# A four-layer network on one core: the third layer's experts are no longer stepped while its gates are computed

## The chip, the cores and the metric

The kernel runs on one core of a Trainium2 chip. The core has five engines with an instruction queue each, worked off in order: TensorE (PE; its weight loads are shown apart as PEld), VectorE (DVE), ScalarE (ACT), GpSimd (POOL) and SyncE (SP), which here only issues DMAs. ACT issues a few DMAs as well. The metric is the device time of one execution in microseconds (us), lower is better. The median of three runs before the change is 3140.76 us (3139.37 to 3149.32).

## The reference, cut to what matters

The network has four layers on x, 4096 tokens of 128 values (in the third layer seen as 4 sequences of 1024, as 4 rows b of 8 tiles of 128 tokens in the kernel). Each layer computes a sequence branch s and a gate branch g from the normalised x:

```python
xn = layernorm(x)
s  = attn(xn)          # layers differ: state space, entmax, rotating state, relative attention
g  = silu(ffn(xn))     # layers differ: fp4, two mixtures of experts, int8
x  = x + s * g
```

Only the third layer (index 2 in the code) is touched. Its sequence branch is a recurrence: per token and head a 2x16 state is turned by an angle, decayed, corrected along a key, and read with a query:

```python
Sd   = rotate(S, ct, st)                    # ct, st from the gates: softplus, tanh, sqrt, ln, exp ...
pred = einsum('bhsd,bhd->bhs', Sd, kt)
S    = Sd + bt * (vt - pred)[..., None] * kt
```

Its gate branch is a mixture of 8 experts (two chosen per token) and a shared expert. An expert is up-projection, relu, square, down-projection. The two branches need nothing of each other until x + s * g.

## The kernel before, in words

**Order of the work.** The program is written with Python generators that are stepped by hand. A list scheduler at build time then gives each engine one fixed order of instructions; what was written earlier has the higher priority, but an instruction may stand ahead of an earlier one whose inputs the scheduler expects later. At run time each queue is strictly in order, so an instruction that waits holds up everything behind it on its engine.

**The third layer** (`layer2`) has these stages, with their times in the profile: projections; the *gates* (`gates2`, from about 1450 us); the *tables* (`chunks2`, the first from 1583 us); the *scan* (`scan2`, its chunks from 1652 to 1995 us); then the output (`out2`) and the fourth layer.

- **Gates** (`gates2`, L1222 on). All gate values of the layer lie in 128x512 tiles. DVE, POOL and ACT hand the tiles to each other in one long chain; then the angles are multiplied up in prefix products (`turn`, L1230 and L1310, L1312 on DVE), and the results transposed. At 16 places it calls `next(beside, None)`.
- **Grams** (`grams2`). Products of neighbouring keys for the first two tables: POOL multiplies (`gram`, L1459), DVE sums (`A`, L1442). POOL also builds decay factors F (L1423, L1427).
- **Experts** (`experts2`, `moe2`). Row by row (b = 0 to 3): load xn (L1049, a DMA issued from ACT's queue, into one buffer), transpose it (xnT: DVE L115, ACT L117), score and choose two experts (ACT L1071; DVE L1072, L193, L194; POOL L197, L198; DVE L199, L201, L1074), and then two halves of 512 tokens. In each half every expert takes one step: POOL weighs the tokens (`xs`, L1083, two buffers), PE transposes (L1090), ACT copies (`xin`, L1092), PE up-projects (L1112), ACT applies Relu and Square in two parts each (`h`, L1113 and L1114), PE down-projects (L1101, L1102). A half ends with the shared expert (`hs`: ACT L1123, POOL L1124), a copy (`gT`, L1130) and Silu (L1134). The generator yields 26 times a row, 104 times in all.
- **Tables** (`chunks2`). For each of four column groups n: keys times decay (`KT`, L1498, on DVE for n = 0 and on POOL after), then seven pairs of large DVE operations (`more`, L1542, and `KT`, L1543). For n = 2 and 3 the grams are made here (POOL L1523, DVE L1513). `KT` and `kh` have one buffer each; DMAs carry the results to memory (`ktd`, `kdd`) and back (`ktc`, `kdc`).
- **Scan** (`scan2`). 128 chunks of 8 tokens, 16 to a tile i. A chunk is four small DVE operations that depend on each other: `prod` L1664, `w` L1667, `step` L1670, `st` L1675. After every second chunk ACT copies the table columns of two chunks into the state tile (`st<-kdc`, L1644, called `bring`; below: the hand-over copy). The copy can start once the `step` of one odd chunk is done and must be done before L1675 of the next odd chunk. Tile by tile the states are then rebuilt: POOL `kt<-kt,w` (L1606), DVE one long scan (`kt<-mz,kt`, L1615), ACT `last` and `mz` (L1617, L1601), POOL `kt<-kt,qt` (L1618), 16 PE matmuls (L1623), ACT `o` (L1625).

**Who steps the experts.** The generator `beside()` in `layer2` (L983) steps `experts` and `grams` once each; `gates2` calls it 16 times. `scan2` gets `experts` itself (as its argument `beside`): it steps it once for each of the nine steps of the first table, then once per chunk, and drains the rest at its end. So before the change the 104 expert steps are written as 16 in the gates, 9 in the first table and 79 in the scan (to chunk 79).

Of the kernel before, what the change touches and what calls it, by code (L numbers as in the profile page):

```python
# [89 lines left out]
def drain(gen):  # L90
    for _ in gen:
        pass
# [838 lines left out]
def layer2(k, W, x_all, eps5, ps, banks, x3, whole, last, I, first):  # L931
# [6 lines left out]
    with tc.tile_pool(name="l2", bufs=1) as keep, tc.tile_pool(name="l2dram", bufs=1, space=DRAM) as dram:  # L938
# [12 lines left out]
        with tc.tile_pool(name="l2g", bufs=1, side="right") as gp:  # L951
            raw = {
                "V": gp.tile([P, 32, 32], F32, tag="V", name="V"),
                "G": gp.tile([P, 7, 32, 16], F32, tag="G", name="G"),
                "N": gp.tile([P, 2, 32, 16], F32, tag="N", name="N"),
            }
            with tc.tile_pool(name="l2p", bufs=1) as p1, tc.tile_pool(name="l2pd", bufs=2) as p2:
                xn = p1.tile([P, NB * NT, D], F32, tag="xn", name="xn")

                def norm(b):  # L960

                    nc.sync.dma_start(out=xr[:, tokens(b), :], in_=x_all[:, tokens(b), :])
                    var, rs = k.layernorm(p2, x_all[:, tokens(b), :], xn[:, tokens(b), :], eps5)
                    nc.sync.dma_start(out=xd[:, tokens(b), :], in_=xn[:, tokens(b), :])
                    ms = p2.tile([P, NT], F32, tag="ms", name="ms")
                    nc.vector.tensor_tensor(ms, var, rs, ALU.mult)
                    nc.vector.tensor_tensor(ms, ms, rs, ALU.mult)
                    nc.vector.tensor_scalar(ms, ms, 1e-6, None, op0=ALU.add)
                    nc.scalar.activation(ms, ms, AF.Sqrt)
                    nc.vector.reciprocal(ms, ms)  # L970
                    return ms

                project2(k, W, p1, p2, ps, xn, norm, rd, szd, kd, qd, raw)
            banks.close()
            ps = PsumTags(banks, tc, {"mm": 3, "tr": "mm", "o": 2, "st": 2, "A": 1}, "ps2s")
            f1 = late.enter_context(tc.tile_pool(name="l2f", bufs=1))
            f2 = late.enter_context(tc.tile_pool(name="l2fd", bufs=2))
            experts = experts2(k, W, f1, f2, ps, xd, gd)
            early = {}
            with tc.tile_pool(name="l2m", bufs=1) as mp, tc.tile_pool(name="l2y", bufs=2) as yp:  # L980
                grams = grams2(k, f1, mp, yp, ps, kd, early)

                def beside():  # L983

                    while True:
                        next(experts, None)
                        next(grams, None)
                        yield

                gates2(k, W, mp, ps, raw, cosp, sinp, outg, coef, beside(), lambda: decays2(k, f1, coef, early))  # L990
                drain(grams)
# [50 lines left out]
def experts2(k, W, p1, p2, ps, xd, gd):  # L1042

    nc = k.nc

    def load(b):
        if b < NB:
            xn = p1.tile([P, NT, D], F32, tag="xn", name="xn")
            nc.scalar.dma_start(out=xn, in_=xd[:, b * NT : (b + 1) * NT, :])  # L1049
            return xn  # L1050

    xn = load(0)
    for b in range(NB):
        xnT = p1.tile([P, T], F32, tag="xnT", name="xnT")
        k.transpose_tiles(ps, "tr", [xn[:, t, :] for t in range(NT)], xnT)
        yield
        g = p1.tile([P, NT, D], F32, tag="g", name="g")
        yield from moe2(k, W, p1, p2, ps, xn, xnT, g)
        xn = load(b + 1)
        nc.scalar.dma_start(out=gd[:, b * NT : (b + 1) * NT, :], in_=g)  # L1060
# [335 lines left out]
def decays2(k, f1, coef, early):  # L1396


    gp = k.nc.gpsimd
    new = lambda name, shape: f1.tile(shape, F32, tag=name, name=name)  # L1400
    m = by_chunks(coef["decay"])
    pre, post, whole = new("pre", [P, 512]), new("post", [P, 512]), new("whole", [P, 512 // CH])
    gp.memset(pre, 1.0)
    gp.memset(post, 1.0)
    for t in range(1, CH):
        gp.tensor_tensor(by_chunks(pre)[:, :, t], by_chunks(pre)[:, :, t - 1], m[:, :, t - 1], ALU.mult)
    gp.tensor_tensor(whole, by_chunks(pre)[:, :, CH - 1], m[:, :, CH - 1], ALU.mult)
    gp.tensor_tensor(pre, pre, coef["scale"], ALU.mult)
    F = factors2(k, f1, coef, slice(0, P))
    for t in range(CH - 2, -1, -1):  # L1410
        gp.tensor_tensor(by_chunks(post)[:, :, t], by_chunks(post)[:, :, t + 1], m[:, :, t + 1], ALU.mult)
    early.update({"pre": pre, "post": post, "whole": whole, "F": F, "f1": f1})
# [18 lines left out]
def grams2(k, f1, p1, p2, ps, kd, early):  # L1431


    nc = k.nc
    early["A"] = []
    waiting = []

    def reduce():

        while waiting:  # L1440
            to, prod = waiting.pop(0)
            k.tc.keep_in_program_order(nc.vector.tensor_reduce(to, prod, AX.X, ALU.add))  # L1442

    for n in range(2):
        bank = (f1 if n else ps).tile([P, NC * CH * (CH - 1) // 2], F32, tag="A", name="A")
        kh = p1.tile([P, 16, P], F32, tag=f"kh{n}", name="kh")
        for hf in range(2):
            fetch2(nc, kh[hf * 64 : hf * 64 + 64], kd, hf * 4 + n)
        yield
        kc = kh.rearrange("p d (c t) -> p c t d", t=CH)  # L1450
        A, end = [], 0
        for u in range(CH - 1):
            left = CH - 1 - u
            A.append(bank[:, end : end + NC * left].rearrange("p (c t) -> p c t", t=left))
            end += NC * left
            for part in range(2):
                cs = slice(part * NC // 2, (part + 1) * NC // 2)
                prod = p2.tile([P, NC // 2, CH - 1, 16], F32, tag="gram", name="gram")[:, :, 0:left, :]
                nc.gpsimd.tensor_tensor(  # L1459
                    prod, kc[:, cs, u + 1 :, :], kc[:, cs, u : u + 1, :].to_broadcast([P, NC // 2, left, 16]), ALU.mult  # L1460
                )
                reduce()
                waiting.append((A[u][:, cs], prod))
            yield
        early["A"].append(A)
    reduce()
    yield
# [926 lines left out]
```

## Time and profile before

The profiled execution took 3140.11 us, of which 3138.4 us are the span of the trace; the 1.7 us between them lie around the span. That execution is 0.65 us under the median of the three runs.

| stretch of the third layer (us) | length | PE | DVE | ACT | POOL |
|---|---|---|---|---|---|
| gates, to the first table's KT (1449.91 to 1582.85) | 132.94 | 44.67 | 98.19 | 47.59 | 98.86 |
| first table, to the first chunk (1582.85 to 1652.12) | 69.27 | 45.55 | 45.77 | 43.16 | 51.92 |
| chunks with tables (1652.12 to 1799.31) | 147.19 | 75.95 | 128.44 | 68.24 | 123.08 |
| chunks 31 to 43 (1799.31 to 1818.45) | 19.14 | 16.84 | 16.86 | 16.52 | 8.40 |
| chunks 44 to 83 (1818.45 to 1916.65) | 98.20 | 71.37 | 67.08 | 62.90 | 54.69 |
| chunks 84 to 127 (1916.65 to 1994.83) | 78.18 | 14.67 | 69.67 | 15.14 | 23.89 |

How to read it: the columns give the busy time of each engine in that stretch, so an engine near the length of its stretch leaves the others little to gain there. Over the whole program no engine is near full (DVE 72%, PE 69%), so the time of a stage is set by who waits for whom. A line of waits reads "engine tile line <- engine tile line: us in total, times, longest"; the instruction on the left stood at the head of its queue until the one on the right was done. A line of the timeline gives start, length, engine, source line, operation, output<-inputs, shapes, count, and in brackets the idle time before it with its releaser. Line numbers in the trace are those of the kernel before.

### The profile page before, as it was taken

The page shows a single profiled execution, that of the slowest core. Times are in us where ns is not written, and L with a number is a line of the kernel's source. Part 1 is how long each engine was busy: PE and PEld are TensorE (multiplying, and loading weights), DVE is VectorE, ACT ScalarE, POOL GpSimd, SP SyncE. Part 2 cuts the span into 40 slices and gives each one's busy share as a digit, 9 for nine tenths or more (in the row PEclk, how much of TensorE's full clock was granted, in tenths as well). Part 3 has the DMA queues.
Part 4 walks back from the last instruction along what each step waited for, and adds up shares of the span by engine and source line. Part 5 has one row for each costly group of instructions (what it writes and reads, how often), then busy time and mean ns, then how long its engine had stood idle before and what let it go on. Part 6 is the DMA issues. An engine that isn't in the chain of part 4 may idle for free. (4 is left out here: it accounts for less than half of the span.)

```text
span 3138.4 us, 48108 instructions
## 1 busy us (share of the span) xinstructions
PE 2160.2 (69%) x17200; PEld 1281.2 (41%) x17201; DVE 2262.5 (72%) x5474; ACT 1565.8 (50%) x3350; POOL 1258.3 (40%) x1154
## 2 busy tenths in 40 slices
PE   5777777577777776794355474456777777877875
PEld 2555555333333232463122232344545544545553
DVE  5555555778888886665868977566788788698777
ACT  3554544333333333434354564136775866775773
POOL 3433434144433335225778853332233332323322
PEclk9888888588888887896555666675766676766666
DMA  3000000100000000222055365448678688678772
GB/s 78 17 1 1 1 1 1 36 0 0 0 0 0 7 7 7 94 96 66 0 143 131 95 175 127 121 134 281 182 240 276 179 261 262 206 239 275 220 246 66
DMA packets 334388, 335.26 MB, mean 107 GB/s; under 512 B 26032, under 2 KB 307500, under 8 KB 328260
## 3 DMA queue, kind: packets, MB, share of 16 engines
q1 hardware_dynamic: 332996, 328.00, 35.6%
q10 hardware_dynamic: 1152, 4.19, 0.4%
q8 instruction: 135, 2.21, 0.3%
q14 instruction: 105, 0.86, 0.1%
HBM read 177.40 MB, written 154.14 MB: 106 GB/s over the span
## 5 line engine op out<-in xcount | busy, mean ns | idle before, releaser
L2252 ACT ACTIVATE neg<-neg,low 128x640 f32<-128x640 f32 (+7 forms) x512 | 390.8, 766 | 102.5 <-DVE low L2245 101.5
L1939 DVE STREAM_TRANSPOSE wT<-neg 128x640 f32<-128x640 f32 (+7 forms) x512 | 366.1, 754 | 51.3 <-PE po L2266 47.7
L2196 POOL TENSOR_SCALAR_AFFINE_SELECT rel<-rel 128x512 f32<-128x512 f32 x288 | 179.8, 635 | 555.1 <-DMA rel<-flat 424.1
L2266 PE MATMUL po<-wT,vb 128*32 128x64 f32 (+1 forms) x10240 | 270.6, 256 | 71.5 <-issue 40.6
L2229 PE MATMUL score<-k,q 32*128 32x512 f32 (+3 forms) x768 | 225.4, 598 | 114.2 <-DVE low L2245 113.5
L2266 PEld LDWEIGHTS po<-wT,vb 128*32 128x32 f32 x10240 | 214.7, 137 | 144.4 <-issue 83.9
L2245 DVE CUSTOM_DVE_ANT_0 neg<-score,rel,low 128x128 f32<-128x128 f32 (+3 forms) x448 | 213.1, 510 | 74.1 <-PE score L2229 33.3
L2167 ACT COPY r<-pr 128x512 f32<-128x512 f32 x256 | 135.2, 584 | 137.9 <-PE pr L2165 96.2
L2245 DVE CUSTOM_DVE_ANT_0 neg<-score,rel 128x512 f32<-128x512 f32 (+3 forms) x320 | 150.7, 520 | 47.1 <-issue 23.2
L2229 PEld LDWEIGHTS score<-k,q 32*128 32x128 f32 x768 | 99.7, 252 | 205.1 <-DVE low L2245 132.8
L2165 PE MATMUL pr<-emb,q 32*128 32x256 f32 x512 | 128.6, 438 | 46.8 <-ACT r L2167 25.8
L840 ACT ACTIVATE h<-pg 128x512 f32<-128x512 f32 x128 | 75.9, 596 | 157.9 <-PE pg L837 154.4
L837 PE MATMUL pg<-xnT,w 128*128 128x512 f32 x256 | 149.3, 667 | 7.0 <-DVE h L841 3.9
L790 POOL TENSOR_TENSOR prod<-rest,kv 128x2048 f32<-128x2048 f32 x32 | 145.2, 4574 | 18.4 <-ACT rest L780 18.4
L839 PE MATMUL pu<-xin,w 128*128 128x512 f32 x256 | 140.6, 632 | 12.9 <-DVE h L841 7.4
L828 PE MATMUL po<-h,w 128*128 128x512 f32 x256 | 129.7, 627 | 26.3 <-DVE h L841 26.3
L2165 PEld LDWEIGHTS pr<-emb,q 32*128 32x128 f32 x512 | 92.3, 270 | 80.2 <-ACT r L2167 38.1
L433 PE MATMUL px<-hT,xbcT 128*128 128x512 f32 x256 | 115.1, 594 | 0.0
L785 DVE TENSOR_REDUCE s<-prod 128x128 f32<-128x2048 f32 x32 | 73.1, 2284 | 49.3 <-POOL prod L790 49.3
L1623 PE MATMUL read<-kt,const_sb 128*128 128x128 f32 x256 | 50.6, 369 | 82.7 <-POOL kt L1618 82.7
L2150 POOL COPY vb<-vr 32x1024 f32<-32x1024 f32 x64 | 66.5, 1040 | 79.8 <-PE po L2266 67.5
L1090 PE MATMUL pt<-ident,xs 128*128 128x128 bf16 x256 | 35.4, 290 | 90.7 <-POOL xs L1083 81.5
(648 smaller groups left out, 5849.4 us busy)
## 6 DMA issues: line engine op xcount, KB each, us to landing
flat<-r SPq DMA_DIRECT2D x128, 512.0 KB
rel<-flat SPq DMA_DIRECT2D x112, 512.0 KB
flat<-r SPq DMA_DIRECT2D x128, 256.0 KB
rel<-flat SPq DMA_DIRECT2D x96, 256.0 KB
kt<-kd SPq DMA_DIRECT2D x16, 512.0 KB
kdc<-kdd SPq DMA_DIRECT2D x16, 512.0 KB
qt<-qd SPq DMA_DIRECT2D x16, 512.0 KB
ktc<-ktd SPq DMA_DIRECT2D x16, 512.0 KB
```

The lines of the kernel that those rows point to most:

```text
L790: nc.gpsimd.tensor_tensor(prod, attn.rearrange("p (t h g) -> p t h g", t=4, g=16)[:, t].unsqueeze(2).to_broadcast(each), kv[:, t, 1, :].re ...
L828: nc.tensor.matmul(po, W["w2"][:, e, c, :], h[:, c, :], start=(e == 0 and c == 0), stop=(e == 7 and c == 1))
L837: nc.tensor.matmul(pg, W["w1"][:, e, c * P : (c + 1) * P], xnT, start=True, stop=True)
L839: nc.tensor.matmul(pu, W["w3"][:, e, c * P : (c + 1) * P], xin, start=True, stop=True)
L1939: nc.vector.transpose(weights[at, pair][j][:, t % 2, 0 : (t + 1) * P], S[j][:, 0 : (t + 1) * P])
L2165: nc.tensor.matmul(to[:, m, :], q[at, t * P : (t + 1) * P], W["emb"][at, i, :], start=True, stop=True)
L2167: nc.scalar.copy(r[:, n], to)
L2196: nc.gpsimd.affine_select(out=rel[:, :, slot(back), :], in_=rel[:, :, slot(0), :], compare_op=op, fill=fill, base=0, pattern=[[0, 4], [-si ...
L2229: nc.tensor.matmul(halves[j // 2][:, j % 2, 0 : last - first], q[at(j), 1 + t * P : 1 + n], kk[at(j), first:last], start=True, stop=True)
L2245: nc.vector.tensor_tensor_reduce(out=neg[:, begin:last], in0=sc[:, begin - first : last - first], in1=rel[:, j, slot : slot + (last - begi ...
L2252: nc.scalar.activation(neg[:, 0:n], neg[:, 0:n], AF.Exp, bias=here, scale=-1.0, accum_out=group["sums"][:, j, t : t + 1])
L2266: nc.tensor.matmul(o[32 * j : 32 * j + 32, 2 * pair + m.start : 2 * pair + 2, :], vb[:, kb % 4 * NT + kb // 4, j].rearrange("p a d -> p (a ...
```

## The change

One line of `beside()` goes. The gates still step the grams at each of their 16 places, but no longer the experts; `scan2` is unchanged and takes the experts from their first step.

```diff
                 def beside():
 
                     while True:
-                        next(experts, None)
                         next(grams, None)
                         yield
```

The same instructions are issued, on the same engines and from the same queues. The 104 expert steps are now written as 9 in the first table and 95 in the scan (to chunk 95). All lines of code behind the deleted one have a number lower by one.

## The prediction

> **What bounds the kernel now.** First read: the busy time by stretch, for the six stretches of the third layer and the few us behind the last.
>
> ```profile
> core 0: us, PE busy (x) PEld busy (x) DVE busy (x) ACT busy (x) POOL busy (x), PEclk, DMA share, GB/s
> 1449.91:1582.85 132.94, 44.67 (x152) 22.04 (x154) 98.19 (x157) 47.59 (x84) 98.86 (x89) 0.55 0.04 9
> 1582.85:1652.12 69.27, 45.55 (x143) 17.05 (x141) 45.77 (x29) 43.16 (x86) 51.92 (x31) 0.57 0.62 160
> 1652.12:1799.31 147.19, 75.95 (x255) 31.40 (x254) 128.44 (x212) 68.24 (x139) 123.08 (x75) 0.62 0.42 107
> 1799.31:1818.45 19.14, 16.84 (x42) 4.39 (x41) 16.86 (x54) 16.52 (x35) 8.40 (x7) 0.73 0.91 308
> 1818.45:1916.65 98.20, 71.37 (x267) 35.73 (x268) 67.08 (x170) 62.90 (x131) 54.69 (x40) 0.65 0.54 122
> 1916.65:1994.83 78.18, 14.67 (x78) 14.10 (x77) 69.67 (x180) 15.14 (x39) 23.89 (x15) 0.58 0.52 115
> ```
>
> In the gates DVE and POOL are both busy for three quarters and ACT for a third: a hand-over chain between DVE and POOL, with expert work in between. From chunk 44 to 83 nothing is full, DVE least of all; once the experts have ended (1916.65) DVE is busy for 89%. So I read DVE's waits, gates first, then first table, then the last 128 chunks.
>
> ```profile
> DVE A L1442 <- POOL gram L1459: 18.4, 6, 5.5
> ...
> DVE more L1542 <- POOL KT L1498: 10.1, 1, 10.1
> DVE xnT L115 <- PE pt L125: 9.9, 1, 9.9
> ...
> DVE st L1675 <- ACT st L1644: 22.0, 9, 5.6
> DVE kt L1615 <- POOL kt L1612: 4.0, 1, 4.0
> ```
>
> The gates wait for POOL, whose queue also holds xs. The scan waits for ACT's hand-over copies, whose queue also holds the experts. How such a wait arises is seen on the timelines of ACT and DVE at 1884 to 1895, and how the scan runs free on ACT's at 1925.
>
> ```profile
> 1884.30 0.57 ACT L1092 COPY xin<-pt 128x512 bf16<-128x512 bf16 x1
> ...
> 1886.77 0.58 ACT L1092 COPY xin<-pt 128x512 bf16<-128x512 bf16 x1
> ...
> 1889.24 0.38 ACT L1644 COPY st<-kdc 128x256 f32<-128x256 f32 x1
> ...
> 1889.66 0.31 DVE L1675 TENSOR_REDUCE st<-step 128x16 f32<-128x144 f32 x1 [5.08 <-ACT st L1644]
> 1894.93 0.31 DVE L1675 TENSOR_REDUCE st<-step 128x16 f32<-128x144 f32 x1 [2.44 <-ACT st L1644]
> ...
> 1925.13 0.38 ACT L1644 COPY st<-kdc 128x256 f32<-128x256 f32 x1 [2.56 <-DVE step L1670]
> 1928.06 0.38 ACT L1644 COPY st<-kdc 128x256 f32<-128x256 f32 x1 [2.55 <-DVE step L1670]
> ```
>
> One expert step takes ACT 2.47 us from one xin to the next (1884.30 to 1886.77). Two free chunks take DVE 2.93 us (1925.13 to 1928.06). So one expert step between two copies fits; two do not.
>
> **A rule for the scan, checked on before.** Let w be ACT's expert work between two neighbouring copies, in the queue's fixed order. A copy takes 0.34 us of the queue. A copy that follows a late one is late by w + 0.34 - 2.93. One that follows a copy in time may use both intervals: late by w - 5.1 (2 x 2.93 less two copies). If a long scan (L1615) falls between, 4.2 us more fit. In the order of before, the stretches of the last row's second half hold 9.73 and 4.98 us: the rule gives 4.6 and 2.4, measured are 5.08 and 2.44. It sizes what follows.
>
> **The change part by part.** The sum is made against the profiled execution (3140.11 us, span 3138.4), 0.65 us under the median.
>
> *Removed from the gates.* By the built order, 13 xs leave POOL (at 1.12 mean, 14.4 us), the top-2 pair (1.09 + 1.59) and a hs pair (2.4): 19.5 us. DVE loses xnT, biased, cmp, eq, rank, two and score (4.2 us) and their waits (1.6 + 1.3 + 1.15). ACT loses eight whole expert steps and more, among them those that held up no one. The bounds: 8 us, if DVE alone sets the pace; 20 us, if POOL does. Walking both queues in the new order with the old durations: reciprocal of det 4 us earlier (alpha no longer waits behind the experts on ACT), reciprocal of mag 11 earlier (the POOL add before it stood behind four xs), the second table's first gram 18 earlier (1525.8 to about 1507.5). From there to the last POOL product (u, 1575.03) the order holds the same work; it ends about 20 earlier. Then 2 to 3 us are given back: KT of the first table now stands behind biased of row 0, which needs transposes, router matmuls and a Sigmoid (3 us from xnT to biased at 1615 to 1618). Gain 18 us.
>
> *Added to the first table.* The DMA that loads row 0 keeps its place early in ACT's queue. Row 0 is routed here instead of row 1, so the wait of 9.9 us for xnT goes, which stood there because row 1's xn is loaded only after row 0 has left the buffer. What is late next: rank waits about 5 us, as POOL does F and kh before the top-2; then the KT of table 1 stands behind ten xs on POOL instead of five. Ten xs at ACT's pace take 17.7 us (as at 1840.98 to 1858), so DVE idles about 11 us before `more`, against 10.1 measured now. First chunk at about 1623 instead of 1652: this stretch gains 10.5. Bounds: the whole idle time of DVE here (22.8) and a loss of 3. SP's queue is shifted with its producers; the new order of its DMAs differs only from table 2 on, and I price that at nothing, since ktc and kdc of the early tiles land over 5 us before use.
>
> *Chunks 0 to 30.* Both versions have written 39 expert steps by chunk 30. Row 1's routing meets POOL's KT of table 3 and two grams in front of its top-2 (a rank wait of about 8 us), but L1615 moves out of a crowded place, where it took 6.5 us. I take 0, with 8 either way.
>
> *Chunks 31 to 127.* Here 65 expert steps are left instead of 49, and where before only row 3 ran against bare chunks, rows 2 and 3 do. The new order of ACT's queue holds these stretches between copies: row 2: 8.43, 4.50, 4.98, 3.01, then 11.97, 4.98, 4.98, 3.01; row 3: 17.91, 3.01, then 9.73, 4.98, 4.98, 5.25. The long one spans eight xin and seven expert steps in front of the copy for chunk 81. Worked through with the rule, the long scans at 59 and 91, and xs held behind kt<-kt,w and kt<-kt,qt on POOL:
> - Row 2: 7.5 + 1.9 + 2.4 + 1.1, then 4.5 + 2.4 + 3.3 + 1.0. Its xn is now loaded about 3 chunks before DVE's xnT, which needs 8.3 to 9.7 us after the load (1606.42 to 1614.73; 1815.24 to 1824.9): 5.5. Its rank stands behind kt<-kt,qt on POOL: 3.1. Sum 33.
> - Row 3: xnT 4.4, biased 0.2, then 15.6 for the stretch of 17.91, 0.7, 6.0, 2.3, 1.0. Sum 30.
>
> Before, the waits in this region sum to 26.6 (22.0, and 2.8 + 1.2 + 0.6 for row 3's routing; the 4.0 of L1615 lie behind the last chunk). One more routing on DVE adds 3.4. So this region loses 63 - 26.6 + 3.4 = 40 us. Bounds: 3.4, if row 2 hides as row 2's second half does now (chunks 31 to 43 run at 1.47 us each); 60, if the POOL holds add to each stretch in full.
>
> *Behind the scan* nothing changes but the start: the experts still end some 30 chunks early.
>
> Sum: 3140.1 - 18 - 10.5 + 0 + 40 = 3151.6, so **3152 us**.
>
> **A rule of the skill against the change.** The row first: with the experts among them, the gates keep POOL at 98.86 and ACT at 47.59 of 132.94 us; ACT's share is mostly the experts'. The Trainium skill, Perfetto Trace Analysis, section Optimization Strategy, says that regimes bound by different engines may gain by being interleaved; the change undoes such a mix. Taken plainly, the moved ACT work, about 30 us of those 47.59, would be lost, and the sum would be 3170. The row says that the mix also costs, since POOL is common to both; hence the sum by waits.
>
> The Trainium skill, SBUF — State Buffer, section Who interferes with whom, holds that a two-input DVE operation and a GpSimd read block each other. The trace has the 128x256 product ps at 3.37 us beside its like at 0.41, with grams on POOL. By the rule up to 14 us of xs could also return as DVE time, and the sum would be 3138; no run so far shows how much of it lies on the path.
>
> **The rivals.**
> - *Faster: the scan hides row 2.* The gains in gates and table come, but rows 2 and 3 cost what row 3 costs now. Place: the copies for chunks 51 and 81. For: ACT is idle for 35 of 98 us at chunks 44 to 83. Against: the fixed order puts 8.43 and 17.91 us of work in front of these copies. Time: 3140.1 - 28.5 + 3.4 = 3115. It decides once the extra waits of chunks 31 to 127 stay under 25 us.
> - *Slower by more: the gates are bound by their own chain.* DVE and POOL hand over in turn, so only DVE's 8 us return, the table gains half (5), the scan loses 40: 3167. For: after 1526 DVE is busy for most of the time and waits little. Against: the 18.4 us for grams.
> - *Nothing comes of it.* The gain (28.5) and the loss are of one size; with a loss of 28 the time stays at 3140. For: each stall can be absorbed by slack that the rule doesn't see. Against: the rule was short, not long, in its check.
>
> **How the numbers follow.** Forecast case 0.50 (its own range 3143 to 3164), faster 0.17, slower by more 0.18, nothing 0.15. What a measurement tells from no change is 0.3%, 9.4 us: faster means under 3131.3, slower over 3150.2. Faster: 0.17 + 0.02 of the edge of nothing. Same: 0.13 of nothing and 0.09 of the forecast's lower edge, 0.22. Slower: 0.41 of the forecast and 0.18: 0.59. Range: to 3124 (half way into the faster case) and 3178 (the rival slower by more, 3167, with 11 us more, from the upper bounds 8 and 60), leaving out about 2 in 10.
>
> **What would show it.** Right: the first KT (L1498 on DVE) near 1565, first chunk near 1623, chunk 30 near 1770; last chunk near 2006 (1994.5 now); DVE's waits for L1644 about 45 us instead of 22.4, with one of some 15 us at chunk 81 and one of some 7 at chunk 51. Wrong: no gain at the first KT (gates bound by their chain), or waits for L1644 near 22 (the order of ACT's queue doesn't bite), or a new wait at rank or at L1615 that none of the steps has.

## The result, and the profile after

The changed kernel takes 3177.3 us (median of 4 runs, 3172.58 to 3187.94). The ratio to the kernel before is 1.0116, with a 95% interval of 1.0096 to 1.0137: it is slower by 1 to 1.4%. The forecast was 3152 with a range of 3124 to 3178. The sign was right and the range held the time by 0.7 us, but the loss was a third of the one measured (11 us against 32 between the medians of four runs each).

The sum by stages is made between the two profiled executions, 3187.94 and 3140.11 us. The profiled execution of the changed kernel is 10.6 us above its median; a second profiled one (e7 below) took 3187.6 us and shows the same waits, so the stages are read from a repeatable trace. The stages differ by 47.8 us in all, the medians by 32.3: what the shorter executions do differently was not seen, and both traced ones are longer than the three others above (3172.58 to 3181.12), so the sizes below hold for traced executions. One execution, the profiled one of e8 below, took 3997.56 us, and its trace is not read.

| stretch | before | after | difference | forecast |
|---|---|---|---|---|
| gates, to the first table's KT (end) | 1582.85 | 1569.62 | -13.2 | -18 |
| first table, to the first chunk | 69.27 | 59.03 | -10.2 | -10.5 |
| chunks 0 to 30, with the tables | 147.19 | 152.20 | +5.0 | 0 |
| chunks 31 to 127 | 195.52 | 258.15 | +62.6 | +40 |
| behind the last chunk | 1143.6 | 1147.2 | +3.6 | 0 |

The busy time by stretch of the changed kernel shows this: gates, first table, chunks 0 to 30, chunks 31 to 127 (columns as in the view of before: stretch, length, then PE, PEld, DVE, ACT and POOL busy, clock, DMA share, GB/s).

```profile
1449.46:1569.62 120.16, 11.98 (x56) 10.11 (x56) 90.66 (x153) 19.86 (x31) 85.05 (x79) 0.51 0.05 11
1569.62:1628.65 59.03, 29.35 (x75) 8.57 (x76) 44.32 (x27) 25.99 (x52) 44.96 (x22) 0.54 0.64 163
1628.65:1780.85 152.20, 71.18 (x230) 28.88 (x229) 127.12 (x212) 66.46 (x135) 120.30 (x72) 0.55 0.37 96
1780.85:2039.00 258.15, 151.49 (x574) 76.84 (x573) 164.08 (x408) 141.72 (x295) 110.57 (x84) 0.66 0.46 113
```

The same view of before for chunks 31 to 127 as one stretch:

```profile
1799.31:1994.83 195.52, 102.87 (x385) 54.22 (x385) 153.61 (x402) 94.56 (x205) 86.97 (x62) 0.63 0.57 137
```

In the last stretch ACT's busy time grew by 47 us, the moved expert work, and still ACT is idle for 116 of 258 us. DVE's busy time grew by 10.5 us, its idle time by 52. So the place to read is DVE's waits there. Those of the changed kernel, chunks 31 to 127:

```profile
DVE st L1674 <- ACT st L1643: 64.4, 15, 16.9
DVE xnT L115 <- PE pt L125: 12.3, 2, 10.3
DVE rank L199 <- POOL cmp L198: 2.3, 2, 1.2
```

The first line is the hand-over copy (one line number lower than before). It stood at 22.0 us. It grew by 42.4, xnT by 11.7; with DVE's 10.5 us of work and what the waits of biased and rank gave (1.5 less) this is the stretch's loss to within a us. The timeline of DVE gives the three longest of these waits, at chunks 51, 65 and 81:

```profile
1843.53 0.31 DVE L1674 TENSOR_REDUCE st<-step 128x16 f32<-128x144 f32 x1 [10.38 <-ACT st L1643]
...
1888.28 0.31 DVE L1674 TENSOR_REDUCE st<-step 128x16 f32<-128x144 f32 x1 [9.94 <-ACT st L1643]
...
1945.10 0.31 DVE L1674 TENSOR_REDUCE st<-step 128x16 f32<-128x144 f32 x1 [16.93 <-ACT st L1643]
```

The one at chunk 81 was forecast at 15.6 us, that at chunk 51 at 7.5, that at chunk 65 at 2.4. The last is where the forecast fell short most, and the timelines of four engines show why, in order of time:

```profile
1870.60 4.25 POOL L1605 TENSOR_TENSOR kt<-kt,w 128x2048 f32<-128x2048 f32 x1
1874.80 4.51 POOL L1617 TENSOR_TENSOR kt<-kt,qt 128x2048 f32<-128x2048 f32 x1
1879.26 1.05 POOL L1082 TENSOR_TENSOR xs<-xn,score 128x512 bf16<-128x512 f32 x1
1879.36 5.49 PE L1622 MATMUL read<-kt,const_sb 128*128 128x128 f32 x24 [5.27 <-POOL kt L1617]
1884.65 0.63 PE L1089 MATMUL pt<-ident,xs 128*128 128x128 bf16 x4
1885.31 0.59 ACT L1091 COPY xin<-pt 128x512 bf16<-128x512 bf16 x1 [7.39 <-PE pt L1089]
1887.88 0.36 ACT L1643 COPY st<-kdc 128x256 f32<-128x256 f32 x1
```

The copy stands behind one expert step on ACT. That step's xin waits 7.39 us for a transpose on PE. The transpose stands behind PE's reads of the finished states, the reads wait 5.27 us for POOL's product with qt, and xs itself stands behind both products on POOL. Three queues in a row hold a 0.36 us copy on which the scan depends. The rule of the forecast knew ACT's queue only; the forecast had added a hold by POOL at chunk 51, but none here.

### The profile page after: what moved, and what is told of

The parts are those of the page before. It is cut to its first block, busy times and chain, and to the rows that moved or that the text cites. A ratio compares the mean times of both kernels' runs of the same rounds, so it can differ in the third digit from the quotient of the medians.

```text
span 3186.2 us, 48120 instructions
## 1 busy us (share of the span) xinstructions
PE 2162.5 (68%) x17201; PEld 1284.5 (40%) x17201; DVE 2259.9 (71%) x5474; ACT 1565.3 (49%) x3350; POOL 1258.8 (40%) x1154
## 5 line engine op out<-in xcount | busy, mean ns | idle before, releaser
L785 DVE TENSOR_REDUCE s<-prod 128x128 f32<-128x2048 f32 x32 | 73.1, 2284 | 49.7 <-POOL prod L790 49.7
L1082 POOL TENSOR_TENSOR xs<-xn,score 128x512 bf16<-128x512 f32 x64 | 81.6, 1286 | 65.6 <-PE pt L1089 57.1
```

## The experiments

The two theories at the start: (T) what costs the scan is the order of ACT's queue, a copy behind expert work; (R) the amount of expert work beside bare chunks costs, by POOL, PE or collisions, wherever the copies stand. All runs are variations of the changed kernel unless "before" is said.

### e1: the hand-over copies on DVE

```diff
-            nc.scalar.copy(
+            nc.vector.tensor_copy(
                 st[n // 2 % 2][:, :, 0:16, 0:CH],
```

> The changed kernel with the 64 hand-over copies on DVE instead of ACT; nothing else is edited. Theory (a copy that stands behind expert work in ACT's queue is what costs the scan its time): the 64.4 us of waits for the copy go, 64 copies of some 0.4 us (as emb 128x256 from PSUM, 0.41) come on DVE, 26 us: 3177 - 64 + 26 = 3139, between 3129 and 3149. Rival (the expert work itself costs, through POOL, PE or reads that collide with DVE's, wherever the copies stand): the waits turn up elsewhere and the copies come on top, 3190 to 3205.

Measured: 3150.33 us, ratio to before 1.004 (1.0027 to 1.0053), just beyond the upper end of T and far below R. A copy costs DVE 0.43 us, 27 us for 64, and chunks 31 to 127 take 223 us instead of 258. 47 of the 64 stand in that stretch and cost DVE 20 us there. So taking them out of ACT's queue gave 55 us in the stretch (35 and these 20), net of the waits that then came to light. Of DVE's waits in this stretch the largest are now:

```profile
DVE xnT L115 <- PE pt L125: 22.3, 2, 20.0
...
DVE kt L1614 <- POOL mz L1601: 6.3, 1, 6.3
```

DVE reaches row 3's transposes 20 us too early. The load of xn stands in the ACT queue that the experts fill: it is issued at 1870.30, 5.5 us after DVE was ready, and its copy on DVE starts 14.4 us after that. T holds in the main; its forecast was missed by 11 us, and the waits for xnT, 10 us longer in all than in the changed kernel, are those that grew most.

### e2 and e3: the expert steps spread over the whole scan

e2, on the changed kernel (e3, on the kernel before, has `n % 2` for `n % 3`):

```diff
-            next(beside, None)
+            if n < 31 or n % 3:
+                next(beside, None)
```

> The changed kernel, but from chunk 31 on the scan steps the experts after two of three chunks only (95 steps over all 128 chunks instead of 96). The order built for ACT's queue then holds no stretch over 5.6 us between two copies of the last 96 chunks, apart from those that follow a long scan. Theory: the waits for the copy fall from 64.4 to under 20 us, and with the gains ahead of the scan (23 us at the first chunk) the time is about 3130, between 3120 and 3142; the experts end with the scan, so up to 8 us may come back behind it. Rival (it is the amount of expert work against the bare chunks that costs): the amount is the same, 3165 to 3180.

> The kernel before, but from chunk 31 on the experts are stepped after every second chunk only (79 steps over 128 chunks instead of 80). Theory: the 22 us of waits for the copy fall to about 5, 3145 - 17 = 3128, between 3120 and 3136. Rival (amount of work): 3145, between 3140 and 3150. Against the run of the changed kernel with paced experts it tells what the 16 expert steps in the gates cost by themselves: the 18 us that the changed kernel is ahead at chunk 30, if the scan then takes the same time.

Measured: e2 3144.37 us, ratio 1.0006 (0.9994 to 1.0017); e3 3146.25 us, ratio 1.0026 (1.0016 to 1.0037). e2 does the same amount of expert work in the same stage as the changed kernel and gets its whole loss of 1.2% back, which speaks for T and against R. Both are 14 to 18 us slower than T's number, though. In e2, 8 of the 14 lie behind the scan: its last chunk ends 3 us before that of the kernel before (1991.8 and 1994.83), but the rest takes 1151.6 us instead of 1143.6. The waits that remain in e2 (DVE):

```profile
DVE st L1674 <- ACT st L1643: 25.1, 8, 8.8
...
DVE xnT L115 <- PE pt L125: 8.7, 2, 5.5
DVE rank L199 <- POOL cmp L198: 6.9, 2, 5.7
```

Apart from those behind a long scan, no stretch of e2's ACT queue was to exceed 5.6 us, half a us more than the rule allows, and yet 25 us are left, mostly at chunks 51, 63, 79 and 95: all but the first at the ends of tiles, where POOL works on the states. Ahead of the copies for these three ACT itself sat idle for PE, 9.2, 3.0 and 3.1 us in its timeline. In e3 the scan waits 17.6 us for the copies at 51, 79, 95 and 111, 8.7 for xnT and 3.8 for rank; it is no faster than the kernel before. So the waits seem to have a second cause beside the order of ACT's queue; e5 and e11 test it.

### e4: half of the gates' places

```diff
-                    while True:
+                    for n in range(99):
+                        if n >= 8:
+                            next(experts, None)
                         next(grams, None)
```

> The experts are stepped at the last 8 of the 16 places of the gates and not at the first 8. The built order then puts stretches of 12.9 us before the copy for chunk 59 and 18.3 us before that for chunk 73, and nothing over 5.1 elsewhere in the last 96 chunks but 7.3 and 7.5 behind long scans. Theory: waits for the copy of 8 to 12 us at chunk 59 and 13 to 17 us at chunk 73, none over 3 at chunk 81; 28 us by the order alone, up to 45 with POOL's holds; the time about 3158, between 3145 and 3170. Rival (amount of work): half way between the two kernels, 3161, with the waits spread as the work is and no single one of over 10 us at these two chunks.

Measured: 3175.95 us, ratio 1.0118 (1.0103 to 1.0134). The time is off both forecasts: half of the move costs as much as the whole. But the long waits are where the built order puts them, at chunks 59 and 73:

```profile
1866.13 0.31 DVE L1676 TENSOR_REDUCE st<-step 128x16 f32<-128x144 f32 x1 [8.90 <-ACT st L1645]
...
1912.82 0.31 DVE L1676 TENSOR_REDUCE st<-step 128x16 f32<-128x144 f32 x1 [15.15 <-ACT st L1645]
```

All waits for the copy from chunk 31 on come to 47.3 us, 28 to 45 forecast. The single long wait of 16.9 us at chunk 81 has moved to chunk 73 with the stretch; at chunk 81 there are 4.1 us, one more than forecast. A wait of 7.4 us at chunk 51, where ACT's order has little, again follows a tile's end (chunk 47), as the product on POOL does. The first chunk comes 12 us earlier than before, chunk 30 3 us earlier, and the scan then takes 32 us more. The loss is a matter of where stretches happen to fall, and does not go with the number of steps moved.

### e5 and e11: the holds on POOL and PE taken away

e5 leaves out fifteen sixteenths of the two state products on POOL; e11 leaves out 15 of the 16 reads of each tile as well.

```diff
-            by_chunk(hist), by_chunk(kt), w[:, :, 0:CH].unsqueeze(1).to_broadcast([P, 16, NC, CH]), ALU.mult
+            by_chunk(hist)[:, 0:1], by_chunk(kt)[:, 0:1], w[:, :, 0:CH].unsqueeze(1).to_broadcast([P, 1, NC, CH]), ALU.mult
...
-        nc.gpsimd.tensor_tensor(hist, hist, qt, ALU.mult)
+        nc.gpsimd.tensor_tensor(hist[:, 0:1], hist[:, 0:1], qt[:, 0:1], ALU.mult)
...
-        for d in range(16):
-            nc.tensor.matmul(po, k.ident, hist[:, d, :], start=(d == 0), stop=(d == 15))
+        for d in range(1):
+            nc.tensor.matmul(po, k.ident, hist[:, d, :], start=(d == 0), stop=(d == 0))
```

> The changed kernel with the two state products on POOL (kt<-kt,w and kt<-kt,qt, 4.2 and 4.5 us each) cut to a sixteenth of their elements: the other fifteen sixteenths of both products are left out. The order of ACT's queue stays the same but for one copy that moves by two small instructions. Theory (xs stood behind these products on POOL, xin behind xs, the copy behind xin): the wait at chunk 65 falls from 9.9 to about 2.5 us and that at chunk 51 from 10.4 to about 5, while those whose stretch holds no such product stay: about 16 us at chunk 81 and 5 at chunk 89. Waits for the copy in all about 48 instead of 64.4; two-input operations of DVE no longer meet the products (biased 4.0 to 0.2 us); the last 9 us of POOL behind the scan go. Time 3177 - 16 - 4 - 9 = 3148, between 3140 and 3158. Rival (these waits come from PE's pace or from the order alone): the waits at chunks 51 and 65 stay over 8 us, and only the end behind the scan goes: 3168.

> As e5, and 15 of the 16 matmuls for each tile's read are left out as well, so that neither POOL's two state products nor PE's reads (5.5 us, which stood in front of the transposes of xs in PE's queue) hold up the experts. Theory (at chunk 65 the hold ran from POOL's product over PE's reads to the transposes, xin and the copy): the wait there falls from e5's 5.1 to 2.5 us or less, which is what the rule gives from ACT's order alone, those at chunks 97 and 99 (3.0 in e5) to under 1; those at 81 (16.7) and 89 (6) stay, and the waits for the copy come to about 46 us in all. Rival (5.1 is the experts' own pace on PE): no change at chunk 65.

Measured: e5 3144.6 us (3148 forecast), e11 3127.75 us (one execution each side in e11, 3149.51 for the kernel before beside it). Both leave work out, so their times are not gains; the waits are what is compared. e5's trace is of its longest execution (3161.05 us), and the 9 us that were to go behind the scan are not seen in it (1148.3 us there, 1147.2 in the changed kernel). The waits for the copy, e5 first, then e11, each with the line of chunk 65:

```profile
DVE st L1675 <- ACT st L1644: 52.1, 15, 16.7
...
1864.51 0.31 DVE L1675 TENSOR_REDUCE st<-step 128x16 f32<-128x144 f32 x1 [5.11 <-ACT st L1644]
```

```profile
DVE st L1675 <- ACT st L1644: 43.6, 14, 13.4
...
1856.95 0.31 DVE L1675 TENSOR_REDUCE st<-step 128x16 f32<-128x144 f32 x1 [2.36 <-ACT st L1644]
```

At chunk 65 the wait goes 9.94, 5.11, 2.36, and the last is what the rule gave from ACT's order (2.4). Chunk 51 goes from 10.38 to 5.40 and 4.79, and the pair at 97 and 99 from 4.57 to 3.0 and 0.3. All waits for the copy go 64.4, 52.1, 43.6: about 21 us of the 64 are holds on POOL and PE, and 44 stay when these are gone. DVE's busy time in the stretch falls by 7.4 us in e5 as well. Chunk 81, forecast to stay, fell to 13.4 in e11; the rule alone gives 12.8 for its stretch of 17.91 (17.91 - 5.1). At chunk 51 the rule alone gives 3.3, and 4.8 are left. So the holds are shown by e5 and e11, and that ACT's order makes waits by e2 and e4; that all of the 44 is order is the rule's reading of the list.

### e7: the changed kernel once more

> The changed kernel as it is, once more. Theory (the waits follow from the built order of ACT's and POOL's queues): the same chunks wait, within 1 us each, 62 to 66 us in all. Rival (the waits came by chance, as from DMAs that were late in that execution): other chunks or other sums, by more than 5 us.

Measured: 3187.6 us; 64.4 us of waits for the copy again, at chunk 51 10.36 (10.38), at 65 9.93 (9.94), at 81 16.69 (16.93), at 95 and 99 2.2 and 3.0 where it was 0.8 and 4.6. Two chunks (95 and 99) moved by 1.5 us, over the 1 us that the theory gave them, and the wait for xnT is 14.9 us instead of 12.3. e12 below, whose edit lies in the gates, waits 65.2 us, at the same chunks but for 2.2 us at chunk 33. The waits follow from the built order, not from chance.

### e6 and e8: steps kept away from the holds

The experts say whether the next step is a heavy one, and from chunk 31 on such a step is written only at seven chunks of a tile (e6). e8 also makes the copy `o<-read` on DVE.

```diff
-            next(beside, None)
+            if n < 31 or not heavy:
+                heavy = next(beside, None)
+            if n >= 31 and heavy and c in (1, 3, 5, 7, 9, 11, 12):
+                heavy = next(beside, None)
...
-        nc.scalar.copy(o[:, at], po)
+        k.tc.keep_in_program_order(v.tensor_copy(o[:, at], po))
```

> The changed kernel, but from chunk 31 on an expert step is written only at seven of the sixteen chunks of a tile (1, 3, 5, 7, 9, 11 and 12), so that none is due while POOL works on the state products; the small steps between halves and rows go on at every chunk. Theory: the stretches of ACT's queue stay as short as in the version with two of three chunks, and the xs that stood behind POOL's products are gone too: waits for the copy about 10 us instead of 25.1, rank's wait about 2 instead of 6.9; the wait for the late xn stays. Time 3144 - 18 = 3126, between 3118 and 3140. Rival (what is left in the scan does not come from the hold on POOL): 3140 to 3150.

> The changed kernel with the expert steps spread as in e6, and with the eight copies o<-read made on DVE, eight chunks into a tile, instead of on ACT. Theory (what was left in e6 were copies for the states that stood behind o<-read in ACT's queue, which waits for 16 matmuls and these for the product kt<-kt,qt): the waits of 7.5, 7.3, 4.7 and 8.9 us go, eight copies of 0.3 us come on DVE: 3144 - 28 + 2 = 3118, between 3110 and 3128. Rival (PE's reads hold up the experts' transposes in any case): the waits move to the next chunks, 3138 to 3146.

Measured: e6 3144.46 us, ratio 1.0014 (1.0001 to 1.0026); e8 3150.18 us, ratio 1.0028 (1.0011 to 1.0045). Both rivals were nearer in time. In e6 the copies wait at chunks 63, 79, 99 and 111. ACT's timeline ahead of the copy for chunk 63:

```profile
1857.23 0.27 ACT L1624 COPY o<-read 128x128 f32<-128x128 f32 x1 [5.26 <-PE read L1622]
1858.54 0.59 ACT L1122 ACTIVATE hs<-ph 48x512 f32<-48x512 f32 x1 [1.04 <-PE ph L1121]
1859.04 0.67 ACT L1643 COPY st<-kdc 128x256 f32<-128x256 f32 x2
```

I took the first of these lines for the cause and moved `o<-read` in e8, which gained nothing. The second line points to what moving it leaves: in e6's trace the experts' matmul stands on PE behind the same reads, which end at 1857.20. That this is what held e8 is not shown, since e8's waits are not known.

### e13: spread steps without the holds

e6 with what e11 leaves out.

> The spread expert steps of e6 with the parts left out that e11 leaves out (fifteen sixteenths of POOL's two state products and 15 of 16 reads of each tile). Theory (a scan whose expert steps are spread loses its time only to the holds on POOL and PE): the waits for the copy fall from 28.9 to under 5 us, the last chunk comes 30 us earlier than in e6, near 1967, and the time is 3144 - 30 - 9 = 3105, between 3095 and 3118. Rival (expert steps cost the scan in another way too, as by their own length on PE): copy waits stay over 12 us, 3120 to 3135.

Measured: 3109.28 us, ratio 0.9889 (0.9872 to 0.9906), with work left out; the last chunk's L1676 starts at 1968.83. Both are near T's numbers. The waits for the copy are not:

```profile
DVE st L1676 <- ACT st L1644: 16.1, 4, 5.6
```

16.1 us instead of under 5, at chunks 51, 63, 79 and 111. The time was reached because other things fell too: chunk 30 came 8.5 us earlier than in e6, and DVE met fewer products. ACT's timeline tells what stands ahead of the four. Ahead of the copies for chunks 51, 63 and 111 (10.5 us of the 16.1) ACT works without a gap for 5.6 to 6.8 us, at 111 from the first line to the second, so the spread order still holds stretches that are too long there. Ahead of the one for chunk 79 ACT is idle: it waits 4.81 us for the shared expert's matmul on PE (line of the second fence), and PE had waited 2.83 us for `hs` on POOL.

```profile
1933.91 0.22 ACT L1617 COPY last<-kt 128x16 f32<-128x16 f32 x1 [1.80 <-DVE kt L1615]
...
1940.74 0.68 ACT L1644 COPY st<-kdc 128x256 f32<-128x256 f32 x2
```

```profile
1877.73 0.58 ACT L1129 COPY gT<-po 128x512 f32<-128x512 f32 x1 [4.81 <-PE po L1127]
```

This is read from the trace; no run changed it.

### e9 and e10: the kernel before with o on DVE

The second edit of e8, on the kernel before (e9) and on e3 (e10).

> The kernel before with only the eight copies o<-read moved to DVE. Theory: of its 22 us of waits for the copy those at chunks 63, 79, 83 and 99 have o<-read or its neighbours in the stretch, at most 8 us; those at 65, 73 and 75 (13 us) are expert work and stay: 3141 - 6 + 2 = 3137, between 3131 and 3143. Rival (o<-read is behind all of them): 3141 - 20 = 3121.

> The kernel before with the expert steps after every second chunk from chunk 31 on, as in e3, and the eight copies o<-read on DVE. Theory: of e3's 17.6 us of waits for the copy nearly all go, the late xn (8.7) stays: 3146 - 15 = 3131, between 3124 and 3138. Against e8 it tells what 16 expert steps in the gates cost when neither scan has stretches that are too long: e8 ahead by 10 to 18 us (its first chunk comes 23 us earlier, its scan has 16 steps more). Rival: both within 5 us of each other.

Measured: e9 3145.94 us, ratio 1.0018 (1.0004 to 1.0032); e10 3144.62 us, ratio 1.0009 (0.9994 to 1.0025). Neither gains; both theories were missed. In e9 the waits for the copy fall from 22.0 to 18.7 only. In e10 they were to go nearly all and are 22.3 us, where e3 had 17.6; only the late xn (8.7) is gone. e8 was to be 10 to 18 us ahead of e10 and is 5.6 behind: with spread steps, 16 steps in the scan cost about what they cost in the gates (e2 and e3, spread steps without the second edit, lie 1.9 us apart).

### e12 and e14: four buffers for gram

This asks where 5 us of the gates' forecast went. e12 is the edit on the changed kernel, e14 on the kernel before.

```diff
-            with tc.tile_pool(name="l2m", bufs=1) as mp, tc.tile_pool(name="l2y", bufs=2) as yp:
+            with tc.tile_pool(name="l2m", bufs=1) as mp, tc.tile_pool(name="l2y", bufs=4) as yp:
```

> The changed kernel with four buffers for gram instead of two. Without xs POOL waits for DVE's sums A in the gates (3.2 and 2.4 us in front of two grams), since a gram needs a free buffer. Theory (the 5 us that the gates gained less than forecast are POOL's new waits for a free gram buffer): these two waits go, the reciprocal of mag starts 3 to 5 us earlier than 1483.7 and the first KT 3 to 6 us earlier than 1569.6. Rival (the decay products pre, post and F are slower beside a busier DVE, 0.80 instead of 0.41 us each, and take back what is gained): mag may come earlier, but the first KT stays within 2 us of 1569.6.

> The kernel before with four buffers for gram instead of two. Theory (POOL waits for a free gram buffer in the gates of both kernels, 17.4 us before and 22.5 after): the first KT comes 3 to 5 us earlier, and nothing behind it changes: 3137, between 3133 and 3140. Rival (xs fills these waits of POOL in the kernel before): no change, 3139 to 3143.

Measured: the first KT of e12 and, below it, of e14:

```profile
1564.81 2.28 DVE L1497 TENSOR_TENSOR KT<-kh,pre 128x2048 f32<-128x2048 f32 x1
```

```profile
1577.99 2.28 DVE L1498 TENSOR_TENSOR KT<-kh,pre 128x2048 f32<-128x2048 f32 x1
```

Both are 4.8 us earlier than without the edit (1569.62 and 1582.85), so the buffers cost both kernels about the same and do not explain the difference between them. In e12 the reciprocal of mag starts at 1483.44 instead of 1483.69: that part of the theory fell, the gain comes behind it. Of the two waits in front of mag one went (2.4 us) and one stayed (3.2), and mag did not come earlier for it. e14 takes 3135.18 us, ratio 0.998 (0.9969 to 0.999): it is faster than the kernel before by 0.2%. e12, one execution of 3188.95 us, shows no gain at the end.

## Why the prediction was right or wrong

**What bounds the kernel.** Right: the copy for L1675 is what the scan waits for, and the longest wait stands where the longest stretch of ACT's queue stands (chunk 65 is the exception, see below). Chunk 81 was forecast at 15.6 and measured 16.9, the group at chunks 53 to 57 at 5.4 in all and measured 5.3, that at 89 and 91 at 8.3 and measured 7.5.

**Removed from the gates, -18.** Measured -13.2, inside the bounds of 8 and 20. The steps were forecast at 4 (det), 11 (mag) and 18 us (first gram of the second table) and came out at 2.6, 7.0 and 10.3. Walking the queues with old durations left out two things that the trace shows. First, POOL's freed time became waits for DVE: for a free gram buffer it waits longer than before (first line; before in the second fence).

```profile
POOL gram L1458 <- DVE A L1441: 22.5, 8, 6.7
```

```profile
POOL gram L1459 <- DVE A L1442: 17.4, 6, 7.6
```

Second, the small decay products on POOL take twice the time where DVE is busy beside them. Before, DVE stood waiting in that stretch; after, it works:

```profile
1510.53 0.42 POOL L1406 TENSOR_TENSOR pre<-pre,decay 128x64 f32<-128x64 f32 x1
```

```profile
1504.36 0.79 POOL L1405 TENSOR_TENSOR pre<-pre,decay 128x64 f32<-128x64 f32 x1
```

The block from the first of them to the next large gram took 16.6 us before, with one xs of 1.4 in it (1506.68 to 1523.25), and 15.6 after, without (1497.38 to 1512.97): this took back half a us. e12 shortens the waits for a buffer (15.4 instead of 22.5) and moves the first KT by 4.8 us, but e14 does as much for the kernel before, and the 4 us that were missing at mag already (7.0 instead of 11) do not come back in e12. So neither of the two is shown to be the missing 5 us; where they lie stays open.

**First table, -10.5.** Right: -10.2. DVE waited 11.7 us for `more`, forecast 11; the wait of 9.9 for xnT is 0.6; rank waited 2.5, forecast 5. Ten xs took 19.3 us, forecast 17.7, so the closeness of the sum is in part luck.

**Chunks 0 to 30, 0.** +5.0, within the 8 given. rank waits 5.1 us, forecast 8; the long scan, which has left its crowded place, takes 5.1 us instead of 6.5.

**Chunks 31 to 127, +40: the step that failed.** Its mechanism was right, its size was not. The waits were forecast at 63 and measure 79; DVE's own work at +3.4 and measures +10.5. In its terms:

- Copies: 24.1 and 25.6 us for rows 2 and 3, measured 33.7 and 30.8. The missing 15 us stand at chunk 51 (7.5 forecast, 10.4 measured), chunk 65 (2.4 and 9.9) and chunk 99 (none and 4.6). I put holds of POOL into the value only at some chunks (7.5 at chunk 51, where the rule alone gives 8.43 - 5.1 = 3.3) and left the others to the upper bound ("60, if the POOL holds add to each stretch in full"); chunk 65 got the bare 2.4. And I did not see that PE's reads stand between the products and the transposes. e5 and e11 take these holds away and leave the rule's number at chunk 65.
- xnT: 5.5 and 4.4, measured 10.3 and 2.1. Row 2's load was issued at 1796.35, and PE's transposes waited for it until 1809.37, 13 us; the forecast took 8.3 to 9.7 from issue to xnT on DVE, and it was 15.0. The DMA engines were busy for 91% of chunks 31 to 43 in the kernel before and 92% in the changed one, and both load a row at the end of them. In the kernel before the load came 5.5 us after the last transfer that SP had issued (1815.24 and 1809.74), and PE had it 6.4 us later; in the changed kernel it came 1.6 us after it (1796.35 and 1794.71). That the transfers in front made the difference fits this, and no run tested it.
- DVE's work: one routing more is 3.4 us where nothing collides. Two small operations met POOL's products. The timelines of POOL and DVE at chunk 44:

```profile
1816.72 4.50 POOL L1617 TENSOR_TENSOR kt<-kt,qt 128x2048 f32<-128x2048 f32 x1 [18.75 <-ACT last L1616]
1817.26 4.04 DVE L1071 TENSOR_TENSOR biased<-score,ebias 128x64 f32<-128x64 f32 x1
```

The 128x64 addition takes 4.04 us instead of 0.23 and ends about when the product does. `two` (L201) behaves alike in row 3: it takes 3.58 us where it takes 0.18 in row 2. In e5, with the products cut, `biased` takes 0.22 and `two` 0.18 us, and DVE's busy time in the stretch is 7.4 us lower. The forecast had this product as a wait of 3.1 us for rank; rank waited 1.2. The Trainium skill, SBUF — State Buffer, section Who interferes with whom, says that a DVE operation with two SBUF inputs contends with a GpSimd instruction that reads SBUF; `biased` agrees. I had used that rule for the gates, where it was to return up to 14 us to DVE; there DVE's busy time fell by 7.5 us (98.19 to 90.66), 4.2 of it the routing that left, so at most 3.3 are left for it. Its price lay in the scan, where I had not looked.

**The rule against the change.** The advice of the Trainium skill on interleaved regimes (Perfetto Trace Analysis, section Optimization Strategy), as the forecast priced it, gave 3170, and that number was nearer than mine. The runs do not bear out the way it came about: the moved work need not be lost, since e2 does all of it in the scan at 3144. So that it was nearer counts as luck.

**The rivals.** The faster one failed at its own condition: the extra waits of chunks 31 to 127 had to stay under 25 us and were 53 (79.2 less 26.6). "Bound by their own chain" gave 3167, nearer than the forecast, but not by its mechanism: the first KT gained 13.2 us, half way between its 8 and the 18 of the forecast, and the table gained 10.2, not 5. "Each stall can be absorbed by slack that the rule doesn't see" is the opposite of what happened: what the rule did not see were further queues.

**Slips in the working.** In chunks 44 to 83 POOL is the least busy engine (54.69 us), not DVE (67.08). By chunk 30 the kernel before has written 55 expert steps; 39 holds for the changed one. The forecast waits for the copy add up to 49.7 us (24.1 and 25.6), while the sign to look for says 45. None of the three changes the sum.

## What to carry to other kernels

Price a moved step on every queue that feeds it, and not only on the queue where the waiting instruction stands: here a 0.36 us copy was late because of reads on PE, one queue away from ACT, and products on POOL, two queues away. Where a chain of small operations depends on copies in a shared in-order queue, list the work between neighbouring copies in the built order and compare it with the time between them; that told beforehand which chunks would wait (59, 73, 81). Work out such a list for both versions of a kernel before moving work from a stage with idle engines to another one: the free time of an engine in the new stage (116 of 258 us here) says little while its order is fixed.

## What was not expected

- The loss does not grow with the steps moved: 8 of 16 steps cost as much as 16 (3175.95 and 3177.3 us), since it depends on where long stretches and tile ends meet.
- The waits are nearly deterministic: two executions agree within 0.25 us at 13 of the 15 waiting chunks, while the executions of one kernel range over 23 us (the kernel before, 3130.82 to 3153.46 beside e8 to e10).
- POOL's own operation is held by DVE as well: in the changed kernel `cmp` (L198) at 1910.52 took 5.26 us where it took 1.26 at 1823.97, beside a long scan on DVE (4.98 us from 1909.74).
- Two more buffers for gram, which no step of the prediction spoke of, make the kernel before faster (0.998, 0.9969 to 0.999).
